# The second-order attention of a fused layer: u transposed through VectorE and DRAM, the work behind it moved a step later, feed-forward weights parked in DRAM, and one set of row sums for q, k and v

## The chip, the cores and the metric

The kernel runs on one core of a Trainium2 chip. The metric is the device time of one execution in microseconds (us); a median of several runs is given. Engines are named as in the profile: PE (TensorE, the matrix unit; PEld are its weight loads), DVE (VectorE), ACT (ScalarE), POOL (GpSimd) and SP (SyncE, which here only issues DMA transfers). PE, DVE, ACT and POOL each work through their instructions in the order in which the kernel gives them.

## The reference, cut to what matters

Input x is (2, 2048, 256), float32. Four residual layers follow one another, each on a layer norm of x: a gated linear scan, a feed-forward layer with ternary weights (256 to 1024 to 256, exact gelu), an attention of second order, and the same feed-forward layer again.

```python
x = x + scan_layer(layernorm(x))
x = x + ffn(layernorm(x))          # w1, b1, gelu, w2, b2
x = x + hla(layernorm(x))          # W_q, W_k, W_v, W_o
x = x + ffn(layernorm(x))          # the same weights
```

The attention has 16 heads of 64 features and is causal. For each head, with q, k and v of time t:

```python
G    = G + k_t (k_t . C)           # C before this time step
S    = S + k_t k_t^T
C    = C + q_t v_t^T
o_t  = q_t . (S C - G)
```

The kernel computes it in two linear attentions, one after the other: u of a time is the causal sum over earlier keys, u_t = sum over i <= t of k_i (k_i . q_t); and o_t = sum over i <= t of v_i (u_i . q_t), where u takes the place of the key. For chunks of 128 times this becomes small matmuls: a part from the state before the chunk (inter), a part inside the chunk (products, masked, then intra), and an update of the state.

## The kernel before, in words

x stays in SBUF as 32 tiles of 128 rows x 256. The first stage (front, up to about 325 us) computes the scan layer and the first feed-forward layer block by block; the second (attention, about 325 to 1055 us) the attention; the third the second feed-forward layer. All 256 x 1024 products are done by Strassen's scheme in the form of Winograd, seven half-size products in place of eight: sums of quarters of the weights are made once (weights_kv, weights_q, ffn_weights_in and _out, on POOL), sums of quarters of the rows for each block.

**Steps.** The attention has 32 steps, s = 0 to 31; step s is chunk n = s // 2 of batch b = s % 2. In the comments here an even step is one with b = 0 (first in the code). q, k and v are made for a pair of steps at once, from xnT, the transposed normed rows of both batches. Class Seven holds the seven products of one of them; go(2, 1, 0, 5, 6, 7, 3, 4) emits them: products 1, 6, 7 and 4 add up in one PSUM bank X, 5 and 3 in a bank Z, 2 lies in a bank Y. After 1, 6 and 4 ACT copies X away, after 7 DVE adds X to another quarter; the next product into X must wait for that copy or sum. k of the next pair is made in the even steps, q and v in the odd ones.

What a step s does, in this order, is written out by hand in the loop of attention (L963 to L1048); the order within each of PE, DVE, ACT and POOL is that of the code:

- inter(s, "S", "uT") and products(s, "kT", "p1"): 64x64 matmuls of q with the state S and with the transposed keys kT; two masked products go to the tile p1 (DVE, L827)
- outward(s - 2, 1): half of the output product with W_o, and the sum into x (L901)
- intra(s, "S", "kN", "p1", "uT"): completes u, transposed (features x times); its two banks are copied to the tile uT by ACT (L859, L861)
- intra(s - 1, "M", "vN", "p2", "oT"): the same for the second attention and the step before; copied to oT by DVE
- keys_in(s + 1): four reads of the transposed keys of the next step (SP, L920)
- products of k, or of q and v; in between units(s): u is transposed by PE (eight transposes of 128x128, L807) and copied by DVE to uN (L808)
- update(s + 1, "kN", "kN", "S") and update(s, "uN", "vN", "M"): the states S and M (sums on DVE, L884)
- more products of q, k, v; keys(s + 1): ACT's copy to kT (L930)
- inter(s, "M", "oT") and products(s, "uT", "p2"), the last product, keys_out(s + 2), outward(s - 1, 0)

**How k is transposed.** keys_out: DVE transposes the 32x32 squares of kN (L908, one instruction for 128x1024) and SP writes the result to DRAM (kD). keys_in: four reads bring it back so that the squares stand in their transposed places (kR). keys: ACT copies kR to kT, with features and heads in order. kR shares its room with p1.

**PSUM.** Eight banks: a ring of four ("ps"), two for uT and for k's X and Z (or q's), two for oT and for v's.

**The last steps.** Steps 30 and 31 have no next pair. In its place stand products of the second feed-forward layer's first block (class Last: begin, fill), with 7 of 14 in each step.

**SBUF.** w1, w2 and their sums (w1_s, w2_t3) stay in SBUF from the first feed-forward layer to the second.

Of the kernel before, what the change touches and what calls it, by code (L numbers as in the profile page):

```python
# [43 lines left out]
def kernel(  # L44
# [37 lines left out]
    w1 = const.tile([P, ND, FF], FP, name="w1")  # L82
    w2 = const.tile([P, NF, D], FP, name="w2")
    wq = const.tile([P, ND, H * DK], FP, name="wq")
    wk = const.tile([P, ND, H * DK], FP, name="wk")
    wv = const.tile([P, ND, H * DK], FP, name="wv")
# [5 lines left out]
    w1_s = const.tile([P, 3, HF * P], FP, name="w1_s")  # L92
    w2_t3 = const.tile([P, 3, HF, HD], FP, name="w2_t3")
    wq_s = const.tile([P, 3, HK], FP, name="wq_s")
    wk_t = const.tile([P, 3, HK], FP, name="wk_t")
    wv_t = const.tile([P, 3, HK], FP, name="wv_t")
# [4 lines left out]
    gam = early.tile([P, ND], FP, name="gam")  # L101

# [228 lines left out]

    def weights_q():
        lo, hi = slice(0, HK), slice(HK, H * DK)
        A11, A12, A21, A22 = wq[:, 0, lo], wq[:, 1, lo], wq[:, 0, hi], wq[:, 1, hi]
        S1, S2, S3, S4 = wq_s[:, 0, :], wq_s[:, 1, :], A21, wq_s[:, 2, :]
        nc.gpsimd.tensor_tensor(S1, A21, A22, ALU.add)
        nc.gpsimd.tensor_tensor(S2, S1, A11, ALU.subtract)  # L340
        nc.gpsimd.tensor_tensor(S3, A11, A21, ALU.subtract)
        nc.gpsimd.tensor_tensor(S4, A12, S2, ALU.subtract)
# [189 lines left out]
    def front(scan_pool, ffn_pool, tern_pool, then, later):  # L532
# [90 lines left out]
        for i in range(len(blocks)):  # L623
# [3 lines left out]
            if i > 2 and i - 3 < len(later):  # L627
                later[i - 3]()
            steps = ffn_in(g0, fn.pop(i), hT)
# [65 lines left out]
    def attention(keep, pool, state, squares, last):  # L695
# [11 lines left out]
        def pair_sums(n):  # L707
# [3 lines left out]
            t = pool.tile([P, 4, P], FP, tag="T", bufs=1, name=f"T{n}")  # L711
            l, r = slice(0, P), slice(P, 2 * P)
            x11, x12, x21, x22 = x[:, 0, l], x[:, 1, l], x[:, 0, r], x[:, 1, r]
            for o, a, b_, op in (
                (S[:, 0, :], x21, x22, ALU.add), (S[:, 1, :], S[:, 0, :], x11, ALU.subtract),
                (S[:, 2, :], x11, x21, ALU.subtract), (S[:, 3, :], x12, S[:, 1, :], ALU.subtract),
                (t[:, 0, :], x21, x11, ALU.subtract), (t[:, 1, :], x22, t[:, 0, :], ALU.subtract),
                (t[:, 2, :], x22, x21, ALU.subtract), (t[:, 3, :], x12, t[:, 1, :], ALU.subtract),
            ):
                nc.gpsimd.tensor_tensor(o, a, b_, op)  # L720
            pairs[n] = x, S, t

        class Seven:


            def __init__(self, n, nm, tag):
                x, S, t = pairs[n]
                self.n, self.nm, self.tag = n, nm, tag
                l, r = slice(0, P), slice(P, 2 * P)
                lo, hi = slice(0, HK), slice(HK, 2 * HK)  # L730
                w, c = {"qT": (wq, wq_s), "kN": (wk, wk_t), "vN": (wv, wv_t)}[nm]
                x1, x2, x4 = x[:, 0, l], x[:, 1, l], x[:, 1, r]
                ws = {1: w[:, 0, lo], 7: w[:, 0, hi], 4: w[:, 1, hi]}
                if nm == "qT":
                    self.A = {**ws, 2: w[:, 1, lo], 3: c[:, 2, :], 5: c[:, 0, :], 6: c[:, 1, :]}
                    self.B = {1: x1, 2: x2, 3: x4, 4: t[:, 3, :], 5: t[:, 0, :], 6: t[:, 1, :], 7: t[:, 2, :]}
                else:
                    self.A = {1: x1, 2: x2, 4: x4, 3: S[:, 3, :], 5: S[:, 0, :], 6: S[:, 1, :], 7: S[:, 2, :]}
                    self.B = {1: ws[1], 7: ws[7], 2: w[:, 1, lo], 3: ws[4], 4: c[:, 2, :], 5: c[:, 0, :], 6: c[:, 1, :]}

            def take(self):
                shape = [P, NPR, P] if self.nm == "qT" else [P, H * DK]
                o = [keep.tile(shape, FP, tag=self.nm, bufs=3, name=f"{self.nm}{b}_{self.n}") for b in range(B)]
                for b in range(B):
                    d[B * self.n + b][self.nm] = o[b]
                if self.nm == "qT":
                    lo, hi = slice(0, NPR // 2), slice(NPR // 2, NPR)
                    self.C = {11: o[0][:, lo, :], 12: o[1][:, lo, :], 21: o[0][:, hi, :], 22: o[1][:, hi, :]}
# [4 lines left out]
            def product(self, at, i, tag=None):  # L753
# [6 lines left out]
                if self.nm == "qT":  # L760
                    for j in range(NPR // 2):
                        nc.tensor.matmul(  # L762
                            to[:, j, :], lhsT=self.A[i][:, j * P : (j + 1) * P], rhs=self.B[i],
# [36 lines left out]
        def turned(src, s, nm):  # L800

            b, n = steps[s]
            t = pool.tile([P, NPR, P], FP, tag=nm, bufs=1, name=f"{nm}{b}_{n}")
# [41 lines left out]
        def intra(s, sums, nat, pm, nm, evict):  # L845
# [12 lines left out]
            t = pool.tile([P, NPR, P], FP, tag=nm, bufs=1, name=f"{nm}{b}_{n}")  # L858
            evict(t[:, :, halves[0]], banks[0])  # L859
            for h in range(2):  # L860
                evict(t[halves[h], :, halves[1]], banks[1][halves[h ^ 1], :, :])  # L861
# [42 lines left out]
        def keys_out(s):  # L904

            b, n = steps[s]
            kS = pool.tile([P, NQ, SQ, NPR], FP, tag="uN", bufs=1, name=f"kS{b}_{n}")
            nc.vector.transpose(  # L908
                kS.rearrange("p b j q -> p b q j"), d[s]["kN"].rearrange("t (q b i) -> t b q i", q=NPR, b=NQ)
            )  # L910
            kD = squares.tile([NQ, SQ, NQ, SQ * NPR], FP, tag="kD", bufs=3, name=f"kD{b}_{n}")
            nc.sync.dma_start(out=kD.rearrange("a i b c -> (a i) b c"), in_=kS.rearrange("p b j q -> p b (j q)"))
            d[s]["kD"] = kD

        def keys_in(s):

            b, n = steps[s]
            kR = pool.tile([P, P, NPR], FP, tag="p1", bufs=1, name=f"kR{b}_{n}")
            for b_ in range(NQ):
                nc.sync.dma_start(  # L920
                    out=kR[b_ * SQ : (b_ + 1) * SQ].rearrange("i (a j) q -> i a (j q)", a=NQ),
                    in_=d[s]["kD"][:, :, b_, :].rearrange("a i c -> i a c"),
                )
            d[s]["kR"] = kR

        def keys(s):

            b, n = steps[s]
            kT = pool.tile([P, NPR, P], FP, tag="kT", bufs=1, name=f"kT{b}_{n}")
            act(kT, d[s]["kR"].rearrange("p t q -> p q t"))  # L930
            d[s]["kT"] = kT

        def units(s):
            uT = d[s]["uT"]
            turned(lambda p: uT[:, p, :], s, "uN")
# [16 lines left out]
        keys_in(0)  # L952
# [9 lines left out]
        keys(0)  # L962
        for s in range(NS):  # L963
# [16 lines left out]
            if s == 1:  # L980
                q.go(2)
                v.go(2)
            if s >= 2:
                outward(s - 2, 1)
            intra(s, "S", "kN", "p1", "uT", act)
            if s > 0:
                intra(s - 1, "M", "vN", "p2", "oT", dve)
            if s + 1 < NS:
                keys_in(s + 1)
            if not more:  # L990
                last.begin(first)
                fill = last.fill
                fill(2)
                units(s)
                fill(2)
            elif first:
                k = Seven(n + 1, "kN", "uT")
                k.go(2, 1)
                units(s)
                k.go(0, 5, 6)  # L1000
            else:
                if s > 1:
# [3 lines left out]
                units(s)  # L1006
# [5 lines left out]
            if first and n + 2 < CPB:  # L1012
                xn = norm_rows(norm_pool, pair(n + 2), stats)
            elif s == NS - 4:
# [5 lines left out]
            update(s, "uN", "vN", "M")  # L1020
            if not more:
                fill(2)
            elif first:
                k.go(7, 3)
# [5 lines left out]
            if s + 1 < NS:  # L1030
                keys(s + 1)
            inter(s, "M", "oT")
            products(s, "uT", "p2")
            if not more:
                fill(1)
            elif first:
                k.go(4)
            else:
                q.go(4)
            if not first and n + 2 < CPB:  # L1040
# [4 lines left out]
            if s + 2 < NS:  # L1045
# [169 lines left out]
```

## Time and profile before

| | |
|---|---|
| median of three runs | 1253.58 us (1253.51 to 1254.62) |
| the profiled execution | 1252.95 us |
| its span, first to last instruction | 1251.2 us |
| granted clock of PE | 1.00 of full speed |
| DVE / ACT / POOL busy, of the span | 61% / 40% / 20% |
| data moved by DMA | 52.16 MB, most of it k's squares |
| busy in attention (325 to 1055 us, 730.0 us) | PE 726.9, DVE 454.0, ACT 263.5, POOL 81.1 |

The profile lists, for groups of instructions alike, the line, engine, operation, what is written <- what is read, shapes, the count, then the busy time in us and the mean ns of one, then the idle time of the engine just before them and what ended it. Matmuls overlap one another, so the mean of one is longer than the distance from one to the next; the timeline (start, duration, engine, line, operation) shows the distances. "issue" marks idle time for which no other engine was waited for. "hS <-kN" is a matmul group that writes a bank hS and reads kN; names that begin with h are PSUM banks of the attention or of the hidden layer.

### The profile page before, as it was taken

The page shows a single profiled execution, that of the slowest core. Times are in us where ns is not written, and L with a number is a line of the kernel's source. Part 1 is how long each engine was busy: PE and PEld are TensorE (multiplying, and loading weights), DVE is VectorE, ACT ScalarE, POOL GpSimd, SP SyncE. Part 2 cuts the span into 40 slices and gives each one's busy share as a digit, 9 for nine tenths or more (in the row PEclk, how much of TensorE's full clock was granted, in tenths as well). Part 3 has the DMA queues.
Part 4 walks back from the last instruction along what each step waited for, and adds up shares of the span by engine and source line. Part 5 has one row for each costly group of instructions (what it writes and reads, how often), then busy time and mean ns, then how long its engine had stood idle before and what let it go on. Part 6 is the DMA issues. An engine that isn't in the chain of part 4 may idle for free.

```text
span 1251.2 us, 46884 instructions
## 1 busy us (share of the span) xinstructions
PE 1240.6 (99%) x21492; PEld 1002.6 (80%) x21492; DVE 768.3 (61%) x1343; ACT 497.9 (40%) x878; POOL 244.3 (20%) x427
## 2 busy tenths in 40 slices
PE   9999999999999999999999999999999999999998
PEld 6588877999677787777777777778777788999998
DVE  7965664655565756666666666665665665556654
ACT  4355554543533333333333343333332433444542
POOL 3743133322210110110110110111011020322220
PEclk9999999999999999999999999999999999999999
DMA  9100000000211111111111211211111110000001
GB/s 325 41 1 1 1 1 1 1 1 1 69 53 53 37 55 53 54 54 37 64 44 37 71 37 36 71 37 53 53 37 53 53 37 3 20 32 18 18 18 34
DMA packets 36085, 52.16 MB, mean 42 GB/s; under 512 B 3344, under 2 KB 30736, under 8 KB 35888
## 3 DMA queue, kind: packets, MB, share of 16 engines
q1 hardware_dynamic: 35376, 48.77, 11.5%
q8 instruction: 168, 2.75, 0.9%
q0 software_dynamic: 80, 0.14, 0.1%
q10 hardware_dynamic: 432, 0.26, 0.1%
q14 instruction: 29, 0.24, 0.1%
HBM read 28.19 MB, written 20.97 MB: 39 GB/s over the span
## 4 chain that ended last, share of the span: by engine, by line
PE 97%; DMA 1%; DVE 0%; issue 0%; ACT 0%; SPq 0%; POOL 0%; ACTq 0%; DVEq 0%; POOLq 0%
PE hy L895 9%; PE ox L475 9%; PE hx L384 9%; PE pq L271 6%; PE hp L821 5%; PE hkN_X L767 5%; PE hqT_X L762 5%; PE oz L475 5%; PE hvN_X L767 5%; PE hz L384 4%; PE huT L852 3%; PE hoT L838 3%; PE hS L874 3%; PE huT L838 3%; PE hoT L852 3%; PE hM L874 2%
## 5 line engine op out<-in xcount | busy, mean ns | idle before, releaser
L827 DVE TENSOR_TENSOR p<-hp,mask 128x512 f32<-128x512 f32 x128 | 82.4, 686 | 95.0 <-issue 58.5
L895 PE MATMUL hy<-wo,oT 128*128 128x256 f32 x512 | 123.9, 385 | 0.0
L720 POOL TENSOR_TENSOR S<-xnT 128x128 f32<-128x128 f32 x32 | 14.6, 457 | 547.1 <-ACT xnT L204 529.4
L895 PEld LDWEIGHTS hy<-wo,oT 128*128 128x128 f32 x512 | 93.5, 190 | 18.9 <-issue 6.7
L396 ACT ACTIVATE hT<-hT,b_sb 128x256 f32<-128x256 f32 x192 | 85.3, 500 | 34.0 <-DVE hT L428 32.4
L859 ACT COPY uT<-huT 128x512 f32<-128x512 f32 x32 | 18.7, 585 | 192.8 <-PE huT L852 192.8
L271 PE MATMUL pq<-xnT,wqkva 128*128 128x512 f32 (+1 forms) x216 | 84.9, 547 | 0.8 <-DMA wqkva<-in_wqkva_t_dram 0.4
L884 DVE TENSOR_TENSOR S<-S,hS 128x512 f32<-128x512 f32 x60 | 41.2, 687 | 71.7 <-PE hS L874 68.6
L187 ACT ACTIVATE xn<-x_sb,nb,rs 128x256 f32<-128x256 f32 x124 | 64.8, 592 | 16.4 <-POOL nb L173 16.4
L271 PEld LDWEIGHTS pq<-xnT,wqkva 128*128 128x128 f32 x216 | 40.0, 190 | 37.9 <-issue 34.7
L930 ACT COPY kT<-kR 128x1024 f32<-128x1024 f32 x32 | 66.2, 2069 | 1.7 <-DMA kR<-kD 1.7
L384 PE MATMUL hx<-xT,w 128*128 128x256 f32 x256 | 66.1, 381 | 0.0
L481 DVE TENSOR_TENSOR x_sb<-x_sb,ox 128x256 f32<-128x256 f32 x64 | 26.7, 417 | 63.7 <-PE ox L475 63.7
L908 DVE STREAM_TRANSPOSE kS<-kN 128x1024 f32<-128x1024 f32 x32 | 65.3, 2039 | 0.0
L402 ACT COPY hT<-hx 128x512 f32<-128x512 f32 x32 | 18.7, 585 | 93.3 <-PE hx L384 93.3
L808 DVE COPY uN<-huN 128x512 f32<-128x512 f32 x64 | 41.2, 686 | 23.7 <-PE huN L807 23.6
L384 PEld LDWEIGHTS hx<-xT,w 128*128 128x128 f32 x256 | 47.9, 190 | 6.4
L155 DVE BATCH_NORM_STATS2 st<-x_sb 128x6 f32<-128x256 f32 x128 | 51.4, 402 | 2.5 <-DMA x_sb<-in_x_dram 2.3
L361 POOL TENSOR_TENSOR xT<-xnT 128x256 f32<-128x256 f32 x15 | 10.9, 727 | 212.3 <-ACT xnT L217 212.3
L874 PEld LDWEIGHTS hS<-kN 64*64 64x64 f32 x1984 | 32.7, 134 | 23.8 <-issue 13.2
L859 DVE COPY oT<-hoT 128x512 f32<-128x512 f32 x31 | 21.4, 692 | 45.1 <-PE hoT L852 45.1
L467 DVE TENSOR_TENSOR hS<-hT 128x512 f32<-128x512 f32 x62 | 41.2, 686 | 5.6 <-ACT hT L396 5.6
(212 smaller groups left out, 2863.5 us busy)
## 6 DMA issues: line engine op xcount, KB each, us to landing
kD<-kS SPq DMA_DIRECT2D x32, 512.0 KB, 3.0
kR<-kD SPq DMA_DIRECT2D x128, 128.0 KB, 3.1
out_dram<-x_sb SPq DMA_DIRECT2D x16, 256.0 KB, 2.1
x_sb<-in_x_dram SPq DMA_DIRECT2D x7, 512.0 KB, 8.9
w<-in_w_t_dram SPq DMA_DIRECT2D x2, 512.0 KB, 9.2
w<-in_w_t_dram SPq DMA_DIRECT2D x1, 1024.0 KB, 11.1
wk<-in_w_k_dram SPq DMA_DIRECT2D x1, 1024.0 KB, 10.0
wq<-in_w_q_dram SPq DMA_DIRECT2D x1, 1024.0 KB, 11.1
```

Of the source, the lines that this page charges most:

```text
L271: nc.tensor.matmul(pq[:, :nt], lhsT=wqkva[:, d, col : col + P], rhs=xnT[:, d, :], start=(d == 0), stop=(d == ND - 1),)
L384: nc.tensor.matmul(at[a][:, j, :], lhsT=A[:, f * P : (f + 1) * P], rhs=Bm, start=(new and j == 0), stop=True, skip_group_check=True,)
L396: nc.scalar.activation(out, out if src is None else src[:, j, :], AF.Gelu, bias=b1_sb[:, f : f + 1])
L475: nc.tensor.matmul(banks[name][:, c, :], lhsT=A[f // 2][:, f % 2, c * P : (c + 1) * P], rhs=Bm[:, f, :], start=(new and c == 0 and f == 0) ...
L767: nc.tensor.matmul(to, lhsT=self.A[i], rhs=self.B[i], start=new, stop=True, skip_group_check=True)
L827: nc.vector.tensor_tensor(d[s][nm][:, h], banks[h], mask8, ALU.mult)
L838: nc.tensor.matmul(banks[c][halves[h ^ c], p, :], lhsT=d[s][sums][c][halves[h], p, :], rhs=d[s]["qT"][halves[h], p, halves[c]], start=(p = ...
L852: nc.tensor.matmul(banks[c][halves[h ^ c], p, :], lhsT=d[s][nat][halves[c], feats(h, p)], rhs=d[s][pm][halves[c], h, p, :], start=(d[s][su ...
L874: nc.tensor.matmul(banks[c][halves[h], p, :], lhsT=d[s][left][halves[c], feats(h, p)], rhs=d[s][right][halves[c], feats(h, p)], start=True ...
L895: nc.tensor.matmul(py, lhsT=d[s]["oT"][:, p, :], rhs=wo[:, p, :], start=(p == 0), stop=(p == NPR - 1),)
L908: nc.vector.transpose(kS.rearrange("p b j q -> p b q j"), d[s]["kN"].rearrange("t (q b i) -> t b q i", q=NPR, b=NQ))
L930: act(kT, d[s]["kR"].rearrange("p t q -> p q t"))
```

## The change

In attention, u is transposed as k is. The three functions for k are made general (turn_squares, turn_rows, turn_end; the reads get room of their own, "raw", with two buffers). units_out(s) starts it for u and units_end(s - 1) ends it a step later; only the last step keeps PE's transposes.

What follows u moves by a step: update(s - 1, ..., "M"), inter(s - 1, "M", "oT") and products(s - 1, "uT", "p2") run in step s, intra(s - 2, "M", ...) too, and the halves of outward are those of s - 2 and s - 3. uT gets two buffers, qT and vN four. Copies out of the banks are apart from intra now (evict): those of oT are ACT's, in odd steps DVE's. k's product 6 stands behind the updates (and k's product 7 behind 3). keys_out for an even step moves from the end of the step before last into the odd step, behind its first masks. ACT's normed rows for the pair after next move to the end of the even step.

q's products use the same sums of rows as k and v (S); the second set of sums (t, four POOL instructions for each pair) is gone, and q's weights get the sums that k's and v's have.

To make room, w1, w1_s, w2 and w2_t3 are written to DRAM in the first feed-forward layer (its third block, on SP), and read back on ACT's queue at the ends of steps 28 (w1) and 29 (w2), into the room of k's and v's weights.

After the loop, two more stretches of the second attention are left than before, and the feed-forward products around them move by one.

```diff
+    def ffn_weights_away():
+        for nm, w in (("w1", w1), ("w1_s", w1_s), ("w2", w2), ("w2_t3", w2_t3)):
+            kept[nm] = dram.tile(w.shape, FP, tag=f"d{nm}", name=f"d{nm}")
+            nc.sync.dma_start(out=kept[nm], in_=w)
+    def ffn_weights_back(nm, tag):
+        w = const.tile(kept[nm].shape, FP, tag=tag, name=f"{nm}_back")
+        nc.scalar.dma_start(out=w, in_=kept[nm])
+        return w
...
+        def turn_squares(s, nm, src):
+            b, n = steps[s]
+            sq = pool.tile([P, NQ, SQ, NPR], FP, tag="sq", bufs=2, name=f"s{nm}{b}_{n}")
+            nc.vector.transpose(sq.rearrange("p b j q -> p b q j"), src)
+            dr = dram.tile([NQ, SQ, NQ, SQ * NPR], FP, tag=f"d{nm}", bufs=3, name=f"d{nm}{b}_{n}")
+            nc.sync.dma_start(out=dr.rearrange("a i b c -> (a i) b c"), in_=sq.rearrange("p b j q -> p b (j q)"))
+            d[s]["d" + nm] = dr
+        def turn_rows(s, nm):
+            b, n = steps[s]
+            raw = pool.tile([P, P, NPR], FP, tag="raw", bufs=2, name=f"r{nm}{b}_{n}")
+            for b_ in range(NQ):
+                nc.sync.dma_start(
+                    out=raw[b_ * SQ : (b_ + 1) * SQ].rearrange("i (a j) q -> i a (j q)", a=NQ),
+                    in_=d[s]["d" + nm][:, :, b_, :].rearrange("a i c -> i a c"),
                 )
+            d[s]["r" + nm] = raw
+        def turn_end(s, nm):
+            b, n = steps[s]
+            t = pool.tile([P, NPR, P], FP, tag=nm, bufs=1, name=f"{nm}{b}_{n}")
+            act(t, d[s]["r" + nm].rearrange("p t q -> p q t"))
+            d[s][nm] = t
+        def units_out(s):
+            turn_squares(s, "uN", d[s]["uT"].rearrange("f q (b i) -> f b q i", b=NQ))
+        def units_end(s):
+            turn_end(s, "uN")
...
             if s == 1:
                 q.go(2)
                 v.go(2)
+                keys_out(s + 1)
+            elif s % 2 == 1 and s + 1 < NS:
+                keys_out(s + 1)
+            if s == 2:
+                k = Seven(n + 1, "kN", "uT")
+                k.go(2)
+            if first and s > 0:
+                units_end(s - 1)
+            if s >= 3:
+                outward(s - 3, 1)
+            intra(s, "S", "kN", "p1", "uT")
             if s >= 2:
-                outward(s - 2, 1)
-            intra(s, "S", "kN", "p1", "uT", act)
-            if s > 0:
-                intra(s - 1, "M", "vN", "p2", "oT", dve)
+                intra(s - 2, "M", "vN", "p2", "oT")
             if s + 1 < NS:
-                keys_in(s + 1)
+                turn_rows(s + 1, "kT")
+            evict(s, "uT")
             if not more:
+                if s >= 2:
+                    evict(s - 2, "oT")
                 last.begin(first)
                 fill = last.fill
                 fill(2)
-                units(s)
+                if not first:
+                    units_end(s - 1)
+                    units(s)
                 fill(2)
             elif first:
-                k = Seven(n + 1, "kN", "uT")
-                k.go(2, 1)
-                units(s)
-                k.go(0, 5, 6)
+                if s != 2:
+                    k = Seven(n + 1, "kN", "uT")
+                    k.go(2)
+                k.go(1)
+                if s >= 2:
+                    evict(s - 2, "oT")
+                k.go(0, 5)
             else:
+                if s >= 2:
+                    evict(s - 2, "oT", dve)
+                units_end(s - 1)
+                units_out(s)
+                turn_rows(s, "uN")
                 if s > 1:
                     q.go(2)
                     v.go(2)
                 q.go(1)
-                units(s)
                 v.go(1)
...
             if s + 1 < NS:
                 update(s + 1, "kN", "kN", "S")
-            update(s, "uN", "vN", "M")
+            if s >= 1:
+                update(s - 1, "uN", "vN", "M")
+            if s == NS - 1:
+                update(s, "uN", "vN", "M")
+            elif first:
+                units_out(s)
             if not more:
                 fill(2)
             elif first:
-                k.go(7, 3)
+                k.go(6, 3, 7)
...
             if s + 1 < NS:
-                keys(s + 1)
-            inter(s, "M", "oT")
-            products(s, "uT", "p2")
+                turn_end(s + 1, "kT")
+            if s >= 1:
+                inter(s - 1, "M", "oT")
+                products(s - 1, "uT", "p2")
             if not more:
                 fill(1)
             elif first:
                 k.go(4)
+                if n + 2 < CPB:
+                    xn = norm_rows(norm_pool, pair(n + 2), stats)
             else:
                 q.go(4)
+            if not first and s + 2 < NS:
+                keys_out(s + 2)
+            if first:
+                turn_rows(s, "uN")
...
-            if s + 2 < NS:
-                keys_out(s + 2)
-            if s > 0:
-                outward(s - 1, 0)
+            if s == NS - 4:
+                last.weights("w1")
+            elif s == NS - 3:
+                last.weights("w2")
+            if s >= 2:
+                outward(s - 2, 0)
         last.out()
+        outward(NS - 3, 1)
+        intra(NS - 2, "M", "vN", "p2", "oT")
+        evict(NS - 2, "oT")
+        last.out()
+        inter(NS - 1, "M", "oT")
+        products(NS - 1, "uT", "p2")
+        outward(NS - 2, 0)
         outward(NS - 2, 1)
-        intra(NS - 1, "M", "vN", "p2", "oT", act)
+        intra(NS - 1, "M", "vN", "p2", "oT")
+        evict(NS - 1, "oT")
         last.out()
```

## The prediction

> **What bounds the kernel now.** I read the busy shares and the chain that ended last first, then the groups by line, then the timeline of one pair of steps in the attention stage.
>
> ```profile
> PE 1240.6 (99%) x21492; PEld 1002.6 (80%) x21492; DVE 768.3 (61%) x1343; ACT 497.9 (40%) x878; POOL 244.3 (20%) x427
> ...
> PE 97%; DMA 1%; DVE 0%; issue 0%; ACT 0%; SPq 0%; POOL 0%; ACTq 0%; DVEq 0%; POOLq 0%
> ```
>
> TensorE (PE) is busy for 99% of the span and is 97% of the chain, in every stage: attention (325 to 1055 us) has 726.9 busy of 730. So what is taken off PE is worth its full time, unless PE then waits. I listed the starts of PE's groups in the timeline: beside the steady rhythm only 13 pauses of 0.1 to 0.8 us are left in attention, 6.1 us together, all at groups of 64x64 matmuls.
>
> ```profile
> 719.16 1.04 PE L807 MATMUL huN<-ident,uT 128*128 128x128 f32 x8
> ...
> 720.03 1.02 PE L767 MATMUL hvN_X<-wv,xnT 128*128 128x512 f32 x2
> ```
>
> The eight transposes of u hold PE for 720.03 - 719.16 = 0.87 us, start to next start; the mean of 273 ns in the groups counts overlap and would give too much. I measured all 32 steps in this way: 0.87 or 0.88 in nearly all, 28.0 in sum.
>
> **Part by part.** *Removed from PE:* units() remains only for step 31, so 31 x 0.87 = **27.1 us** go. The q, k and v products keep count and shape (q's operands only swap sides), and the number of 64x64 groups is the same, so nothing else on PE changes.
>
> *Added elsewhere, per step:*
>
> ```profile
> L930 ACT COPY kT<-kR 128x1024 f32<-128x1024 f32 x32 | 66.2, 2069 | 1.7 <-DMA kR<-kD 1.7
> ...
> L908 DVE STREAM_TRANSPOSE kS<-kN 128x1024 f32<-128x1024 f32 x32 | 65.3, 2039 | 0.0
> ...
> L808 DVE COPY uN<-huN 128x512 f32<-128x512 f32 x64 | 41.2, 686 | 23.7 <-PE huN L807 23.6
> ...
> kD<-kS SPq DMA_DIRECT2D x32, 512.0 KB, 3.0
> kR<-kD SPq DMA_DIRECT2D x128, 128.0 KB, 3.1
> ```
>
> u now takes the way of k: one 2.04 us transpose on DVE for two copies of 0.69, one write and four reads on SP's queue, and a copy of 2.07 us on ACT. Of the copies of oT (3 x 0.69 us on DVE), those of even steps go to ACT (3 x 0.58). Both engines have room in the sum (about 11 to 18 us of work in steps of 19 to 25), so what counts is the order in each queue. I walked one pair of steps, time 0 at the end of the step's huT<-p,kN group, durations from these rows.
>
> *Odd step.* ACT: copies of uT 0.3 to 2.0, the new copy of uN to 4.1, q1's copy to 4.7; PE reaches product q6, which waits for it, at 6.4: hidden by 1.7. DVE: masks end at -1.4, the moved transpose of k runs to 0.6, oT's copies from 1.1 (their matmuls end then) to 3.3, u's transpose to 5.3; the next sums of DVE that PE needs come at 9.3. Nothing waits. The bank that v1 needs is free at 1.8, PE comes at 3.8.
>
> *The round trip.* Write 2.9, four issues 1.7, last read 2.9: 7.5 us. In the odd step SP is held first by k's rows (write landed at 3.6, issued to 5.3), so u's rows land at about 13 and are wanted after 18. In the even step u's transpose ends at 9.9 and its rows land at about 18; ACT turns to them at 20.9. Slack 3 us, then q6's 1.7. With the update a step later, this covers it.
>
> *Even step: the new wait.* Here u's transpose stands on DVE between the sums of M and the two sums that product k4 needs (k4 adds into the bank that k7's sum reads).
>
> ```profile
> 701.12 1.16 PE L874 MATMUL hS<-kN 64*64 64x64 f32 x64
> ...
> 702.32 1.48 DVE L884 TENSOR_TENSOR S<-S,hS 128x512 f32<-128x512 f32 x2 [1.36 <-PE hS L874]
> ...
> 703.72 1.47 DVE L884 TENSOR_TENSOR M<-M,hM 128x512 f32<-128x512 f32 x2
> ...
> 705.11 0.68 DVE L772 TENSOR_TENSOR kN<-kN,hkN_X 128x512 f32<-128x512 f32 x1
> 705.70 0.68 DVE L772 TENSOR_TENSOR kN<-kN,hkN_Z 128x512 f32<-128x512 f32 x1
> ...
> 707.09 1.12 PE L767 MATMUL hkN_X<-wk_t,xnT 128*128 128x512 f32 x2
> ```
>
> From the start of hS, DVE is through with S and M at 3.99 (705.11 - 701.12), and PE comes to k4 at 5.97 (707.09). Afterwards PE comes at 5.97 + 0.86 = 6.83, as k6 moves into this stretch (0.86: a 512-wide product between others). How long a transpose holds the next instruction, and what PE does behind it, shows once, at the start of attention, with q in k's place:
>
> ```profile
> 320.02 2.03 DVE L908 STREAM_TRANSPOSE kS<-kN 128x1024 f32<-128x1024 f32 x1
> ...
> 321.91 0.67 DVE L772 TENSOR_TENSOR qT<-qT,hqT_X 128x512 f32<-128x512 f32 x1
> ...
> 322.72 1.13 PE L762 MATMUL hqT_X<-T,wq 128*128 128x128 f32 x8 [0.89 <-DVE qT L772]
> ```
>
> The next sum starts 1.89 later, and PE 0.14 after that sum's end. So: 3.99 + 1.89 = 5.88 (k3's sum), + 0.59 = 6.47 (k7's), + 0.68 + 0.14 = 7.29, against 6.83: **0.46 us** of waiting, in steps 2, 4 ... 28: 14 x 0.46 = **6.4 us**. Bounds: 0 (if the sums of S and M come 0.5 earlier) and 0.6 (the full 2.04). Behind k4 on PE stand outward and the next step, so the wait is not made up. k7 itself waits for k6's copy, now behind oT's copies on ACT: 7.6 against 7.7, just hidden; if that cover goes, up to 0.3 more.
>
> *The first steps.* Step 0 has no M and no follower to do meanwhile: k4 is due 3.76 after hS, while its sum comes at 2.60 + 1.89 + 0.59 + 0.68 + 0.14 = 5.90: 2.1 us. Steps 0 to 2 have four smaller waits (S of pair 1 from POOL 0.35, q6 behind uN's copy 0.4, the bank of q4 0.25, masks behind only one product 0.55). Together **3.7 us**; bounds 1 and 5.
>
> *The last steps.* Steps 30 and 31 fill with feed-forward products. In step 30 oT's copies on ACT stand before the copy that p6 waits for (0.7); u's transpose before p7's sum delays p4 (0.3), and through it two gelus, k's copy of 2.07 and the gelu that frees the bank of the next huT.
>
> ```profile
> 1029.72 0.83 ACT L396 ACTIVATE hT<-hx,b_sb 128x256 f32<-128x256 f32 x2
> ...
> 1030.94 1.16 PE L838 MATMUL huT<-qT,S 64*64 64x64 f32 x64
> ```
>
> Now this gelu ends 0.4 before PE comes. p7's sum ended 2.9 after the start of hM; afterwards 5.1 (one sum of M and the transpose more), so the gelu ends at 9.8 after hM where PE comes at 8.05: 1.8 us. In step 31 uN of step 30 ends on ACT 0.9 after PE wants it, and after the loop two copies of oT are waited for, 0.3 each. **4.3 us**; bounds 2 and 7.
>
> *Weights by way of DRAM.* 3.7 MB out, early, on SP, which then has nothing else to send; and back on ACT's queue at the ends of steps 28 and 29 (an issue costs 0.3 to 0.7 on SP). At the 325 GB/s of the span's first slice the first half takes 5.6 us and shares the engines with u's rows of step 28, whose slack is 4.7: nothing, at most 1. w1 is wanted some 30 us later. The four POOL instructions saved per pair are off the path (POOL 20%).
>
> *Sum.* 27.1 - 6.4 - 3.7 - 4.3 = **12.7 us**. The profiled execution took 1252.95 (span 1251.2 and 1.75 around it): 1240.3. The median of the three runs, 1253.58, lies 0.6 above it: **1241.0**.
>
> **Rivals.**
>
> *A, the transposes go for nothing more.* k4's wait and half of the edges vanish since DVE's queue is a little earlier than worked out: 27.1 - 4.0 = 23.1, so about 1230.5. For it: 0.46 is the difference of two chains of five terms. Against: the row at 322.72, where the same order did stall PE. Chance 0.2.
>
> *B, more pauses.* The 13 pauses carry the mark "issue": no wait on an engine is seen. The page lists 168 instruction packets (2.75 MB) beside the data queue, whose traffic from k's squares doubles. If the pauses double with it, 6.1 us are lost: 12.7 - 6.1 = 6.6, so 1247. Against: they fall at the ends of runs of 64x64 groups, where PE uses up instructions fastest, and several lie where no square is moving. Chance 0.18. [...]
>
> *C, slower: the rows of u late in odd steps.* SP takes its transfers in turn, and its order alone is not written out by hand. If u's rows of an even step stand behind the next write of k's squares, which waits for DVE until 0.6 into the odd step, they land at about 0.6 + 0.3 + 1.7 + 2.9 = 5.5; uN follows at 7.6, q1's copy at 8.2, and q6 (6.4) waits 1.9. Fourteen times this is 27 us: 1241 + 27 = 1268. It makes the kernel slower once the rows land later than 4.6 (0.9 us of waiting in each odd step eats the 12.7). For it: SP's longest waits now are just for that transpose (772 us in all), and everything behind one stands still. Against: k's transfers go in the order of the program. Chance 0.12. [...]
>
> **How the numbers follow.** Forecast 0.5, A 0.2, B 0.18, C 0.12. The range takes in A and B with the bounds of k4 and the edges, and leaves out C: 1228 to 1252. A measurement of this kernel tells about 0.2%, 2.5 us. Faster: forecast, A and most of B, 0.84; within: the end of B, 0.04; slower: C, 0.12.
>
> **What would show it.** Right: huN left with 8 matmuls; hkN_X (k4, even steps) waiting on DVE kN for about 0.5 us, 14 times, and 2 us once near 345; PE's first huT of step 31 waiting on an ACT hT; pairs of steps 1.3 us shorter than the 45.2 to 46.5 of now. Wrong: PE waits on a copy q1 or uN in odd steps with the copy itself waiting for DMA (C), more "issue" before 64x64 groups (B), or no wait at k4 (A).

## The result, and the profile after

The changed kernel took 1244.65 us (median of 4 runs, 1243.99 to 1245.38), the kernel before 1253.55 beside it (4 runs): a ratio of 0.9927, 95% interval 0.991 to 0.9945, so 8.9 us faster. The forecast was 1241.0, with 12.7 us gained. The profiled execution took 1245.38 with a span of 1243.6, which is 7.6 less than the 1251.2 of before; its mean granted clock of PE was 0.997.

From the page of the changed kernel: busy times, the instruction queue q8, and the chain by engine:

```profile
PE 1220.3 (98%) x21244; PEld 978.1 (79%) x21244; DVE 751.0 (60%) x1261; ACT 587.8 (47%) x960; POOL 217.3 (17%) x363
...
q8 instruction: 166, 2.72, 0.9%
...
PE 89%; DVE 5%; issue 3%; ACT 1%; DMA 1%; POOL 0%; SPq 0%; DVEq 0%; ACTq 0%; POOLq 0%
...
L939 ACT COPY uN<-ruN 128x1024 f32<-128x1024 f32 x31 | 64.5, 2080 | 3.0 <-DMA ruN<-duN 2.3
...
L919 DVE STREAM_TRANSPOSE suN<-uT 128x1024 f32<-128x1024 f32 x31 | 63.7, 2054 | 2.0 <-ACT uT L871 1.6
...
duN<-suN SPq DMA_DIRECT2D x31, 512.0 KB, 3.5
ruN<-duN SPq DMA_DIRECT2D x124, 128.0 KB, 3.2
```

PE has 248 matmuls less (21492 - 21244 = 31 x 8, the transposes) and 20.3 us less busy time, but the span fell by 7.6 only: the chain, 97% PE before, now has 5% of DVE and 3% of "issue". The new work costs per piece about what k's does (2.05 and 2.08 us as there, 3.5 and 3.2 us a transfer for 3.1 and 3.0). What PE waits for (engine, tile, line <- who released it: us in total, times, the longest), from the waits of PE in the changed kernel:

```profile
PE hkN_X L773 <- DVE kN L778: 4.9, 13, 2.1
PE hoT L858 <- issue: 2.5, 1, 2.5
PE huT L844 <- ACT hT L402: 1.5, 1, 1.5
PE hx L390 <- issue: 1.2, 1, 1.2
...
PE hM L884 <- issue: 0.9, 1, 0.9
PE huT L858 <- issue: 0.9, 3, 0.4
```

The first row is the forecast wait at k4, the third the forecast gelu of step 31. The second and fourth have no releaser (no engine that PE waited for), and stand in no term of the sum.

Where the 7.6 us come from, by the timelines of both (starts of the group huT<-qT,S of each step; "moved" is work of the second attention that goes from steps 0 to 2 to the end, by its groups; "lost" is what is left when moved work and the transposes are taken out):

| stretch | before | after | moved | transposes | lost |
|---|---|---|---|---|---|
| steps 0 and 1 | 41.28 | 39.05 | -5.98 | -1.74 | 5.5 |
| steps 2 to 27 | 593.99 | 574.36 | -1.92 | -22.6 | 4.9 |
| step 28 | 19.22 | 19.22 | | -0.87 | 0.9 |
| step 29 | 26.82 | 29.71 | | -0.87 | 3.8 |
| step 30 | 19.24 | 21.82 | | -0.87 | 3.4 |
| step 31 to the next feed-forward block | 38.21 | 46.92 | +7.71 | | 1.0 |
| rest | 182.05 | 182.13 | | | 0.1 |

Step 29 is where most of the forecast's error lies. W1 comes back there (the two issues are at 961.41 and 961.81). The timeline of PE, changed kernel (start, duration, idle time before in brackets):

```profile
965.05 1.99 PE L905 MATMUL hy<-wo,oT 128*128 128x256 f32 x8
966.97 1.16 PE L858 MATMUL huT<-p,kN 64*64 64x64 f32 x64
967.95 0.28 PE L858 MATMUL hoT<-p,vN 64*64 64x64 f32 x5
970.72 1.97 PE L858 MATMUL hoT<-p,vN 64*64 64x64 f32 x59 [2.49 <-issue]
972.62 1.78 PE L768 MATMUL hqT_Y<-xnT,wq 128*128 128x128 f32 x8
```

PE stops in the middle of a run of 64x64 matmuls, whose operands are all there, and the two groups behind the stop last 1.97 and 1.78 us, where such groups take 1.1 and 1.16 elsewhere. The same stretch by windows (busy us and instructions of each engine, then the granted clock of PE, the busy share of the DMA engines, GB/s):

```profile
964.00:968.00 4.00, 4.00 (x153) 3.44 (x145) 2.83 (x3) 0.00 (x0) 0.00 (x0) 1.00 1.02 357
968.00:970.70 2.70, 0.23 (x16) 0.10 (x5) 0.67 (x2) 1.74 (x3) 0.00 (x0) 0.97 1.04 261
970.70:972.70 2.00, 1.98 (x60) 1.86 (x60) 0.15 (x1) 0.43 (x1) 0.00 (x0) 0.50 0.59 225
972.70:974.20 1.50, 1.50 (x8) 1.50 (x9) 1.46 (x3) 1.50 (x1) 0.00 (x0) 0.58 0.01 3
974.20:978.00 3.80, 3.80 (x23) 2.78 (x23) 3.52 (x4) 1.37 (x4) 0.00 (x0) 1.00 0.57 183
```

In the first window 276 of PE's instructions start (a window also counts those that are under way from before it), 69 in a microsecond, while the transfer fills the DMA engines (1.02, 1.04); then PE stands for 2.5 us with nothing to do, and starts again at 970.72, about as the transfer ends (its last packet at 971.09). After that the granted clock is 0.50 for 3.4 us (970.6 to 974.0 in finer windows), which by an estimate, half of it, costs another 1.7. The page lists the instruction queue q8 among the DMA queues: its 2.72 MB come to 64 bytes for each of PE's 2 x 21244 matmuls and weight loads, in packets of 16.4 KB, so of 256 instructions. That they are PE's is read from this count; the places of the stops, below, bear it out.

The half clock is also there earlier, at 345.9, behind the 2.12 us wait at k4 in step 0, and again for 3.4 us. These two stops, of 2.1 and 2.5 us, are the only ones of over 2 us in this trace, and it came behind both.

So the theory for the runs: **the return of the weights holds up PE's own instructions, which come by DMA as well; the stop then halves the clock**. With the two waits at k4, in step 0 (2.1, and 1.7 of half clock) and in the even steps (some 4 in all), this is about 13 of the 19.6 us in the last column. Rivals: the pauses come from k's and u's squares, whose traffic doubled; they come from single long packets; any long transfer costs the same, wherever it falls.

### The profile page after: what moved, and what is told of

Its sections match the earlier page's. It is cut to its first block, busy times and chain, and to the rows that moved or that the text cites. A ratio compares the mean times of both kernels' runs of the same rounds, so it can differ in the third digit from the quotient of the medians.

```text
span 1243.6 us, 46457 instructions
## 1 busy us (share of the span) xinstructions
PE 1220.3 (98%) x21244; PEld 978.1 (79%) x21244; DVE 751.0 (60%) x1261; ACT 587.8 (47%) x960; POOL 217.3 (17%) x363
## 3 DMA queue, kind: packets, MB, share of 16 engines
q8 instruction: 166, 2.72, 0.9%
## 4 chain that ended last, share of the span: by engine, by line
PE 89%; DVE 5%; issue 3%; ACT 1%; DMA 1%; POOL 0%; SPq 0%; DVEq 0%; ACTq 0%; POOLq 0%
PE ox L481 9%; PE hy L905 9%; PE hx L390 9%; PE pq L272 6%; PE hqT_X L768 5%; PE hvN_X L773 5%; PE oz L481 5%; PE hz L390 4%; PE hp L827 4%; PE hkN_X L773 3%; PE huT L858 3%; PE huT L844 3%; PE hS L884 3%; PE hoT L858 3%; PE oy L481 2%
## 5 line engine op out<-in xcount | busy, mean ns | idle before, releaser
L188 ACT ACTIVATE xn<-x_sb,nb,rs 128x256 f32<-128x256 f32 x124 | 64.8, 593 | 16.4 <-POOL nb L174 16.4
L939 ACT COPY kT<-rkT 128x1024 f32<-128x1024 f32 x32 | 66.6, 2080 | 2.3 <-DMA rkT<-dkT 2.3
L939 ACT COPY uN<-ruN 128x1024 f32<-128x1024 f32 x31 | 64.5, 2080 | 3.0 <-DMA ruN<-duN 2.3
L919 DVE STREAM_TRANSPOSE skT<-kN 128x1024 f32<-128x1024 f32 x32 | 65.5, 2048 | 0.0
L919 DVE STREAM_TRANSPOSE suN<-uT 128x1024 f32<-128x1024 f32 x31 | 63.7, 2054 | 2.0 <-ACT uT L871 1.6
L804 ACT COPY vN<-hvN_X 128x512 f32<-128x512 f32 x16 | 9.4, 586 | 80.0 <-PE hvN_X L773 80.0
L218 ACT COPY xnT<-pt 128x512 f32<-128x512 f32 x32 | 17.2, 590 | 58.4 <-PE pt L212 50.7
L858 PEld LDWEIGHTS huT<-p,kN 64*64 64x64 f32 x2048 | 34.3, 134 | 13.2 <-issue 7.0
```

Source lines behind the costliest of these rows:

```text
L188: nc.scalar.activation(xn[:, c, :], x_sb[:, g, :], AF.Identity, bias=nb[:, c : c + 1], scale=rs[:, c : c + 1],)
L858: nc.tensor.matmul(banks[c][halves[h ^ c], p, :], lhsT=d[s][nat][halves[c], feats(h, p)], rhs=d[s][pm][halves[c], h, p, :], start=(d[s][su ...
L919: nc.vector.transpose(sq.rearrange("p b j q -> p b q j"), src)
L939: act(t, d[s]["r" + nm].rearrange("p t q -> p q t"))
```

## The experiments

The times, each with its ratio to the kernel before on the same chip:

| run | us | ratio, 95% interval |
|---|---|---|
| e1_k_sums_first | 1242.93 | 0.9920 (0.9904 to 0.9935) |
| e2_weights_in_pieces | 1243.85 | 0.9943 (0.9924 to 0.9962) |
| e3_both | 1238.40 | 0.9882 (0.9867 to 0.9897) |
| e4_long_stores | 1258.94 | 1.0058 (1.0040 to 1.0076) |
| e5_u_early | 1236.00 | 0.9862 (0.9847 to 0.9877) |
| e6_u_early_pieces | 1236.33 | 0.9854 (0.9835 to 0.9873) |
| e7_parking_alone | 1261.17 | 1.0058 (1.0043 to 1.0073) |
| e8_u_by_pe | 1268.61 | 1.0119 (1.0104 to 1.0134) |
| e9_short_packets | 1246.53 | 0.9952 (0.9935 to 0.9968) |
| e10_u_early_return_later | 1231.52 | 0.9830 (0.9817 to 0.9844) |
| e12_best | 1230.46 | 0.9827 (0.9813 to 0.9840) |
| e13_long_stores_few_instr | 1244.47 | 0.9935 (0.9921 to 0.9950) |

### e1: k's sums ahead of u's transpose

```diff
-            elif first:
-                units_out(s)
...
                 q.go(3)
+            if first:
+                units_out(s)
```

> The changed kernel, with u's transpose of even steps put behind the sums of k's products on VectorE. Theory (order on VectorE): the waits of PE on the sum of k before product 4 go: 2.1 us in step 0 and 13 x 0.38 in steps 2 to 26, and in step 30 the wait for the bank (1.5) and for p7's sum (0.2): 1244.65 - 8.7 = 1236. Rival (the wait only moves on): the masks of the second attention come 0.7 us later and u's rows 1.3 us later, and PE waits there instead: 1241 or more, with new waits of PE on masks or on uN.

Undisturbed even steps took 18.43 us for 18.74, so the wait at k4 is worth 0.31 a step, and the wait in step 0 fell from 2.1 to 0.8. But a new one came, in the waits of PE of this run:

```profile
PE hqT_X L768 <- ACT qT L787: 4.3, 1, 4.3
```

In step 1 u's rows of step 0 are now late; ACT's copy of uN waits for them, q1's copy stands behind it, and product q6 waits for that. Step 1 took 27.77 for 23.56, half clock included. This is the mechanism of rival C in the prediction, in one step of 32. The gain of the other steps is eaten: the time is hardly better than that of the changed kernel.

### e2 and e3: the weights back in pieces

The return is cut into 14 pieces of 256 KB, issued one at a time over steps 28 to 31; e3 has the edit of e1 as well.

```diff
-        nc.scalar.dma_start(out=w, in_=kept[nm])
...
+        for c in range(0, o.shape[1], 512):
+            todo.append((o[:, c : c + 512], i[:, c : c + 512]))
...
+            if s > NS - 4:
+                piece()
```

> The changed kernel, with the weights read back in 14 pieces of 256 KB spread over steps 28 to 31, one at a time, in place of four transfers of 0.75 and 1 MB. Theory (the long transfer holds up PE's own stream of instructions): the pause of step 29 (29.7 us for 25.1) and the 1.2 us marked issue in step 30 go: 1244.65 - 5.5 = 1239. Rival (the pause belongs to the place, or to u's rows arriving late, and not to the size of the transfers): no change, 1244 to 1245.

> Both edits together. Theory: the two causes are independent, so the gains add: 1244.65 - 8.7 - 5.5 = 1230.5. Rival: one hides the other, and the time stays near the better of the two, 1236.

e2 took 1243.85, no different from the changed kernel. The pause in step 29 shrank from 2.49 to 1.94, and one of 1.8 us came in step 31. e3 took 1238.4; its step 29 ran clean (25.61), but the late rows of step 1 were there again (a wait of 3.2). Smaller pieces alone don't cure it.

### e4: more long transfers in the middle

Three times, at the ends of steps 8, 14 and 20, W_o (1 MB) is written twice to DRAM, for nothing. 6 MB in all, far from the return of the weights.

```diff
+            if s in (8, 14, 20):
+                for i in range(2):
+                    away = dram.tile(wo.shape, FP, tag=f"dwo{i}", name=f"dwo{s}_{i}")
+                    nc.scalar.dma_start(out=away, in_=wo)
```

> The changed kernel, with W_o (1 MB) written twice to DRAM, for nothing, at the ends of steps 8, 14 and 20 on ACT's queue, 6 MB in all; nothing waits for it. Theory (a long transfer holds up PE's instructions): a pause marked issue of 1 to 4 us behind each of the three places, with nothing else waiting: 1248 to 1256. Rival (the pause of step 29 has to do with the last steps): no change, 1244 to 1245.

1258.94, some 14 us above the changed kernel and above the range that was expected. Steps 9, 15 and 21 took 27.55, 30.04 and 30.08 us for 25.1. The third of the stores, in windows (columns as above) and in PE's timeline:

```profile
795.40:799.40 4.00, 4.00 (x141) 3.33 (x131) 2.69 (x3) 0.00 (x0) 0.00 (x0) 1.00 1.06 348
799.40:802.40 3.00, 0.02 (x2) 0.00 (x0) 0.80 (x2) 0.00 (x0) 0.00 (x0) 1.00 0.98 248
```

```profile
798.51 0.92 PE L858 MATMUL huT<-p,kN 64*64 64x64 f32 x45
802.52 0.50 PE L858 MATMUL huT<-p,kN 64*64 64x64 f32 x18 [3.10 <-issue]
```

It is the picture of step 29, made at will, with data that nobody waits for: 62 instructions started in a microsecond, full DMA engines, then 3.1 us of nothing. The three stops are of 1.6, 3.0 and 3.1 us. The theory stands; what I had left out of its price is the half clock that follows the second and third (0.58 from 802.52 to 806.00).

### e5 and e6: u's transpose straight behind the copies of uT

```diff
             evict(s, "uT")
+            if first:
+                units_out(s)
+                turn_rows(s, "uN")
...
-            elif first:
-                units_out(s)
...
-            if first:
-                turn_rows(s, "uN")
```

> The changed kernel, with u's transpose (and its rows) of even steps straight behind the copies of uT, ahead of the sums of S, where VectorE now stands idle for some 3 us. Theory (only the place in VectorE's queue makes the waits): the wait for k's sum goes from step 0 (2.1 us, and 1.7 more of the half clock behind it), from steps 2 to 26 (13 x 0.31) and with it step 30's 1.7; the rows come earlier, not later, so step 1 doesn't wait for them either: 1244.65 - 9.5 = 1235. Rival (the room is too tight: k's first sum now ends 0.1 us before the update of M needs its bank): a wait of 0.3 in each even step takes the place, 1239 or more.

> The same, and the weights read back in 14 pieces. Theory: gains add, 1235 - 5 = 1230. Rival (pieces hold PE up as much as long transfers, as the profile of the run with pieces alone suggests): 1234 to 1235.

e5 took 1236.0, as expected: DVE is idle at that place, the 12 waits at k4 are gone (even steps 18.43), that of step 0 is 0.8, with no half clock behind it, and the rows are in time. Step 29 still had a pause, of 1.38 us. e6 adds the pieces of e2 and took 1236.33, no better: step 29 ran clean (25.46), and the pause went along with the last three pieces into step 31, where PE's timeline has

```profile
1006.59 0.37 PE L837 MATMUL hp<-qT,kT 64*64 64x64 f32 x2 [2.74 <-issue]
```

So here cutting the transfer moved the stop, to where the last pieces lay beside 64x64 matmuls.

### e7: the parking alone, on the kernel before

The kernel before, with the weights written to DRAM and read back as in the change; u and everything else as before, so the squares' traffic isn't doubled.

```diff
+            if s == NS - 4:
+                last.weights("w1")
+            elif s == NS - 3:
+                last.weights("w2")
```

> The kernel before, with only the parking of the feed-forward weights in DRAM (same transfers, same places, long ones). Theory (a long transfer starves PE's stream of instructions, whatever else the change does): one pause of 2 to 3 us marked issue after the end of step 28, half clock behind it, in all 3 to 6 us more: 1257. Rival (it takes the doubled squares as well): within 1 us of the kernel before.

1261.17, 7.5 us slower than the kernel before on that chip. Steps 29 and 30 took 30.37 and 23.41 us for 26.82 and 19.24. The waits of PE in this run:

```profile
PE hoT L869 <- issue: 3.8, 4, 2.4
PE huT L869 <- issue: 3.0, 3, 2.2
```

One stop for each half of the weights, 2.2 and 2.4 us, and half a clock behind each. The rival of the squares falls: their doubling is not needed for it.

### e8: u by PE again, all else as changed

The changed kernel with PE's transposes of u in every step, and a third buffer for uN and for the reads.

```diff
-                if not first:
-                    units_end(s - 1)
-                    units(s)
+                units(s)
```

> The changed kernel, with u transposed by PE in all steps again, at its old places; everything else as changed (followers a step later, parked weights, one set of row sums). Theory (31 x 0.87 us of PE are what the change gains, the waits behind u's transpose on VectorE what it pays): + 27.1 - 9.5 = 1262, and slower than the kernel before by what parking and the edges cost. Rival (the later followers or the other edits gain by themselves): 1253 or less.

Odd steps took 26.0 for 25.12: 0.87 each, the removed group to the digit. Even steps can't be read, as the copies of uN on DVE made a new wait there (hS on DVE's sum of k, 15 times, 7.0 us), so the 1268.61 are too high as a price of the transposes.

### e9: the same bytes in short packets

The parked weights lie in DRAM in rows of 1 KB, so that store and return go in packets of 1 KB, not 6 to 8 KB.

```diff
...
+            f = w.rearrange(flat).rearrange("p (c e) -> p c e", e=256)
+            kept[nm] = w.shape, flat, dram.tile([f.shape[1], P, 256], FP, tag=f"d{nm}", name=f"d{nm}")
+            nc.sync.dma_start(out=kept[nm][2].rearrange("c p e -> p c e"), in_=f)
```

> The changed kernel with the two parked weights kept in DRAM in rows of 1 KB, so that their store and their return move the same 4 MB at the same moments in packets of 1 KB instead of 6 to 8 KB. Theory one (the return holds up PE's instructions by the sheer volume that stands in the DMA engines before them): steps 29 and 30 stay long (29.7 and 21.8 us), a pause of over 2 us stays, time 1244 to 1246. Rival (an instruction block waits behind single long packets): the pauses of steps 29 and 30 shrink under 1 us, half a clock goes with them, step 29 near 26, time about 1239. A third case: short packets take the engines longer, and the time rises over 1247.

1246.53, and a pause of 3.10 us at 972.69, half the clock behind it. It is not that an instruction block waits for a single long packet.

### e10, e13: the same transfers where PE uses few instructions

e10 is e5 with W1's return issued behind the copies of uT in step 29, so that it falls beside the products of q and v, and W2's at that place in step 31. e13 is the changed kernel with the stores of e4 (W_o, for nothing) at blocks 2, 4 and 6 of the last feed-forward layer.

```diff
             evict(s, "uT")
+            if s == NS - 3:
+                last.weights("w1")
+            elif s == NS - 1:
+                last.weights("w2")
```

> The version with u's transpose and rows right behind the copies of uT (1236.0), and the return of W1 issued after u^T has left PSUM in step 29 and that of W2 after the same point in step 31, in the same two long transfers. Theory (PE starves only where it uses up instructions fast, in the runs of 64-wide products; beside the 512-wide products it uses few, and the same transfer costs nothing there): no pause of PE over 1 us in steps 29 to 31, step 29 near 25.5, time 1232 to 1234. Rival (a long transfer costs PE the same wherever it falls): the pauses move along with the transfers, time 1236 or more; if W2 lands too late for the first block of the feed-forward, a wait on it shows.

> The changed kernel with the same 6 MB of extra stores of W_o to DRAM (written for nothing) as in the run with long stores, which cost 14.3 us there, but put in the last feed-forward stage, at blocks 2, 4 and 6, where PE uses about a quarter as many instructions in a microsecond. Theory (a long transfer costs PE time only where PE uses up instructions faster than the queue that brings them can fill beside the transfer): at most 0.5 us, time 1244 to 1246. Rival (any long transfer holds PE up, or takes its memory's turn): 1255 and over.

e10 took 1231.52: step 29 25.46, step 30 19.25, no pause without a releaser there, clock 1.00. (W2's part falls in step 31 in a mixed stretch, 34 instructions started in a microsecond at a DMA share of 0.71, and PE has none there either.) The transfer in its windows, and that of the first of e13's stores:

```profile
964.00:968.00 4.00, 4.00 (x27) 3.04 (x27) 3.14 (x3) 3.02 (x5) 0.00 (x0) 1.00 0.98 389
968.00:972.00 4.00, 4.00 (x103) 2.69 (x102) 1.52 (x3) 1.17 (x2) 0.00 (x0) 1.00 0.56 192
```

```profile
1084.00:1088.00 4.00, 4.00 (x33) 3.87 (x33) 0.84 (x2) 0.08 (x1) 3.13 (x3) 1.00 0.98 396
```

The DMA engines are as full as in e4 (0.98) and PE is busy for all of the 4.00 us, at 13 and 16 instructions started in a microsecond instead of 62 to 69. e13 took 1244.47 for the 1244.65 of the changed kernel, and from the start of step 31 to the end, where its stores are, 228.9 for 229.1: the 6 MB that cost 14 us in e4 cost nothing here. So what a long transfer cost PE in these runs was set by how fast PE used up instructions meanwhile.

The traces show it directly. They hold each packet of q8 with its start and length, and PE's instructions (weight loads, matmuls and semaphore instructions) can be counted off in blocks of 256. In attention, in the kernel before, the changed kernel, e4, e7 and e9, every stop of PE of 0.15 us or more without a releaser lies within three instructions of the same place in the count, which comes once in 256. Take that place as the end of a block: PE goes on 1.2 to 1.8 us after the end of the packet that came last. (Four stops of 0.2 to 0.6 us in e2, e3 and e6 lie elsewhere.) Times from the start of the block, in us:

| block | run | packet starts | block lasts | stop behind it |
|---|---|---|---|---|
| step 29 | changed, W1 on its way | 3.70 | 3.88 | 2.49 |
| step 29 | e10, the same instructions, W1 later | 0.71 | 3.83 | none |
| step 21 | changed | 1.90 | 3.88 | 0.21 |
| step 21 | e4, the same instructions, a store on its way | 4.70 | 3.88 | 3.10 |
| step 31 | e10, W2 on its way | 3.21 | 9.92 | none |

So beside a long transfer the packet started some 3 us later (3.70 for 0.71, 4.70 for 1.90), and PE stopped where the block was used up before the packet was in. The last row is the test: the packet is nearly as late as in step 29, but has 9.9 us to come in. Beside e13's stores a block lasts 15 to 20 us.

### e12: the best version

e10, with the feed-forward's row sums of step 28 behind product k4 and the copy of uN of step 30 at the top of step 31.

```diff
-            if first and s > 0:
+            if first and s > 0 or s == NS - 1:
                 units_end(s - 1)
...
-            if s == NS - 4:
-                last.rows()
...
+                if s == NS - 4:
+                    last.rows()
```

> The version with the return later, and two waits of the end taken away: the row sums of the feed-forward's first block stand behind the product of chunk 4 in step 28 instead of ahead of it (0.6 us wait of PE on the copy of k), and the copy of u of step 30 is made at the top of step 31 (0.8 us). By the traces of before and after these are worth 1.3 us together, one below the other: 1231 to 1233, 1.3 under the version with the return later. Rival: the waits were cover for others (the copies of step 31 late by as much) and the two versions are within 0.5 us.

Both waits went: step 28 18.43 for 19.22, and from step 31's start to the end 228.9 for 229.7 in e10. The median, 1230.46, is 1.1 below that of e10, but the intervals overlap, so by the times alone the two can't be told apart. Against the kernel before it is 0.9827, 22 us by the medians of that chip, of the 27 that PE gave up.

## Why the prediction was right, and where it was off

The direction, the place and nearly every mechanism were right; 12.7 us were forecast and 8.9 came. By its own steps:

- **Removed from PE, 27.1.** Right: 248 matmuls, 0.87 us in each step (e8's odd steps); 31 x 0.87 is 27.0.
- **Odd step, round trip.** Right: no such wait in odd steps, and u's rows were late for ACT once in 31, by 2.3 us beside the return, which no one on PE noticed. Pairs of steps came to 18.74 + 25.12 = 43.86 for 45.22, 1.36 less; 1.3 was forecast.
- **The wait at k4, 6.4.** Mechanism right, size 0.46 for a measured 0.31. In step 16 of the changed kernel:

```profile
687.88 1.16 PE L884 MATMUL hS<-kN 64*64 64x64 f32 x64
...
691.86 2.07 DVE L919 STREAM_TRANSPOSE suN<-uT 128x1024 f32<-128x1024 f32 x1
...
693.76 0.68 DVE L778 TENSOR_TENSOR kN<-kN,hkN_Z 128x512 f32<-128x512 f32 x1
694.36 0.68 DVE L778 TENSOR_TENSOR kN<-kN,hkN_X 128x512 f32<-128x512 f32 x1
...
695.10 1.12 PE L773 MATMUL hkN_X<-wk_t,xnT 128*128 128x512 f32 x2 [0.24 <-DVE kN L778]
```

From the start of hS the two sums stand at 5.88 and 6.48 and PE goes on at 7.22, where 5.88, 6.47 and 7.29 were worked out. PE itself came 0.15 later than thought (6.98 for 6.83); its weight load for product k7 had waited for ACT's copy, the cover that the prediction called thin. Steps 2 to 27 lost 4.9 us, where 13 x 0.46 = 6.0 were given.
- **The first steps, 3.7.** They lost 5.5. The wait at k4 of step 0 was 2.12 for 2.1 forecast, and that for the sums from POOL 0.17 for 0.35; q6, with 0.4 forecast, came only 0.15 late. The 1.7 of half clock behind k4's wait was no term of the sum, and neither was 0.67 at q1 in step 1, whose bank ACT was still copying to uT.
- **The last steps, 4.3.** Steps 28 to 31 lost 9.1. 5.4 of it are the return's: 2.49 and 1.23 of pauses, and 1.7 of half clock. Another 3.1 are the waits that were named (the gelu 1.48 for 1.8, p4 0.22 for 0.3, uN 0.76 for 0.9) and one that wasn't: 0.6 in step 28, where the feed-forward's row sums stand ahead of k's copy on ACT. The last 0.6 I can't place. The waits at p6 and behind the loop did not come.
- **Weights by way of DRAM: "nothing, at most 1".** This is the step that failed. It asked whose data the transfer would delay, found slack, and did not ask what else comes by DMA. In this run it cost 5.4, alone 7.5 (e7).
- **Rival B** had that mechanism (its pauses are stops at the ends of blocks, as above), but tied it to the squares. In steps 2 to 27 the excess of the steps over the undisturbed ones is 6.1 us before (593.99 - 13 x 45.22) and 6.1 after (574.36 + 1.92 - 13 x 43.86): twice the squares, no more pauses in sum, though two single stops of the changed kernel reached 0.93 and 0.96 us, where 0.53 was the longest before. **A** came true only when the order was changed for it (e5). **C** came in one step of e1.

The same return gave pauses from 1.4 to 3.1 us in step 29 of different runs because the packet started 3.2 to 4.7 us into its block. Open: why it is held up for longer in one run than in another, and where it waits; the late packets themselves take 0.9 to 1.5 us, no longer than those of the kernel before (0.9 to 1.7).

## What to carry to other kernels

When a kernel is bound by PE, add its instructions to the DMA budget: a transfer of a megabyte that nobody waits for belongs beside large matmuls, not beside runs of 64x64 ones (the same 6 MB cost 14 us in e4 and nothing in e13). Moving work from the bound engine pays its full time only in the steps where the new work's place in the other engine's queue was chosen for it (e5: the same instruction, a few places earlier, 8 us). And price a stop of PE by what may follow it: behind most of those of over 2 us here, 1.7 more (3.4 us at a clock of 0.50).

## What the runs showed of the hardware

- PE starved for instructions in these runs: stops of 1.2 to 3.1 us without a releaser, in or shortly behind runs of small matmuls. Ahead of those of over 2 us that the windows show (the changed kernel, e4, e7, e9) the DMA engines' share was 0.93 to 1.12 for some 4 us, in which PE used up a block of 256 instructions (3.8 to 3.9 us); at 0.98 with 13 to 16 instructions in a microsecond there was none (e10, e13).
- PE's instructions came in packets of 16.4 KB, by the count 256 in each. The stops without a releaser (attention; the kernel before, the changed kernel, e4, e7, e9) lie within three instructions of one place in that count, and PE went on 1.2 to 1.8 us after the end of the late packet.
- Most stops of PE of over 2 us, whatever they waited for, and one of 1.8 (e2) brought the granted clock to 0.50 for 3.4 us, in two runs for 6.8 (behind 2.74 in e6 and 3.14 in e13). One of 2.13 (step 0 of e13) and one of 3.22 (step 1 of e3) did not, nor did those of 1.73, 1.94 and 1.96 (e8, e2, e1) and those of 1.6 and less. So length alone did not decide; what else did, the runs don't show.
